# Retuning a planned instruction order: nine z buffers, new cost estimates, later table changes, and later state sums in a fused scan, attention and expert kernel

## The chip, the core and the metric

The kernel runs on one core of a Trainium2 chip. The metric is device time in microseconds (us), as the median of several executions. TensorE is called PE here (PEld its weight loads), VectorE DVE, ScalarE ACT, GpSimd POOL, and SyncE SP; SP issues nearly all DMAs.

## What is computed

The input is x, four images (batches) of 384 channels by 32 x 32 points. Two layers follow each other.

```
# layer 0: selective scan over 4 traversals k of the image
xs    = cross_scan(group_norm(x))                       # L = 1024 steps
dt    = softplus(dtw @ (xw_dt @ xs) + bias)             # per channel d
h     = h * exp(dt * A[n]) + (dt * xs) * B[n]           # 16 states n per channel
y     = sum_n h[n] * C[n]  (+ D * xs), merged over the 4 traversals
x     = x + gelu(layer_norm(y))
# layer 1: tokens
t     = t + attention(layer_norm(t))                    # 6 heads, window of 64, causal
t     = t + sum over the top 2 of 4 experts of gate * (gelu(t' w1 + b1) w2 + b2)
```

## The kernel before, in words

**The scan.** One slot of the scan is 128 rows (32 channels by 4 states) by 1024 time steps. There are 768 slots: 4 batches, 4 traversals, 12 blocks of 32 channels, 4 groups of 4 states. For each slot there is a chain:

- `times_b` (L808): POOL multiplies `dtu` (dt times x, spread to 128 rows by a DMA) with the B rows into a buffer `z`.
- `decay` (L824): ACT makes `dA` = exp(dt * A) into PSUM, out of the spread `dts`. There are two `dA` buffers.
- `scan` (L850): DVE runs the recurrence with dA and z. If the planner finds POOL less loaded than DVE, the result goes back into z and POOL multiplies it with C; if not, it goes into dA and DVE multiplies it with C into z (`times_c`, L837).
- `fold_y` (L884): for each pair of slots, once both products with C are ready, four matmuls with `fold` sum the states into PSUM (`ps_y`). After four such pairs DVE adds the running sum `yp`, which is stored again. Only after its fold is a z buffer free.

The spreads `dtu` and `dts` come by `spread` (L798): a 512 KB DMA from a DRAM copy `dtr`, one for each block of 32 channels, and one buffer each; slots alternate between the two blocks of a pair, so two of the four buffers of each kind are in use at a time and two can be loaded ahead. `time_steps` (L741) makes dt with matmuls (`ps_dt`) and ACT's Exp and Ln.

**The tokens and the experts.** When all of a batch is scanned, `tokens` (L961) does attention in tiles of 128 tokens, three at a time, `route` (L1203) picks two experts for each token, and `experts` (L1317) runs 19 blocks of 128 tokens through one expert each: four chunks of 9 matmuls `ps_hid`, three gelus on ACT (`hs`), and 3 matmuls `y_ff`. There are 76 such blocks in all. `combine` (L1409) gathers and adds the result. This work of batch b runs beside the scan of batch b+1 and later; that of the last batch, and what is left over, runs after the scan.

**What sets the order.** All of these are Python generators. The `Machine` (L211) plays them through while the program is built: each operation gets an estimated cost from `Engine.ask` (L154), each engine has a clock, and of the operations that are ready the one with the best time and bias goes out next (`choose`, L322). The chip then runs each engine's instructions in exactly that order, with semaphores between engines; a wrong estimate shows as an engine that waits at the head of its queue. Rules that the change touches:

- PE costs (L177 to L181): 0.00176 us a column; a fold matmul (32 output rows) 0.01 + 0.00022 n; a matmul with fewer than 32 input rows (`ps_dt`) 0.6 of the normal cost. All PE costs grow by `COLD` = 1.9 (L371) while the planned PE load of a stretch of 3.413 us is under a third; `asked.work` (L196) says how much a matmul counts for that load.
- ACT costs (L183): 0.08 + 0.00085 n, and 0.1 more for each operand that is a tensor.
- `PATIENCE` (L369): ACT takes first what needs the function table that is loaded; an operation that needs another table is let in when it has waited this long, or when nothing else is ready. Exp, Ln and Gelu have a table each.
- `settled` (L257): work that asks for it isn't ordered before the planner's clock is within `SOON` = 0.5 us of the time at which its inputs are estimated to be written. `three`, `hidden`, `combine` and `fold_y` (L897) ask for it.
- Stocks of buffers (L511, L512): `NZ` = 7 z buffers, four `dtu` and four `dts`, all of 128 x 1024 float32. `AHEAD` = 3: z is made at most three slots ahead of the scan.

Of the kernel before, what the change touches and what calls it, by code (L numbers as in the profile page):

```python
# [17 lines left out]
P = 128  # L18
B, D, HH, WW = 4, 384, 32, 32
L = HH * WW  # L20
# [22 lines left out]
HID_RANK = 2  # L43
GELU_BIAS = EARLY
FAVOUR = 1.0
TILES, EPS, NZ = 3, 1e-5, 7
CORES = 1
NEG = -1.0e30

# [80 lines left out]
class Engine:  # L130
# [23 lines left out]
    def ask(self, op, a, k):  # L154
        aps = [v for v in list(a) + [v for n, v in k.items() if n not in ("out", "accum_out")] if hasattr(v, "tensor")]
        if "out" in k:
            outs, ins = [k["out"]], aps
        else:
            outs, ins = aps[:1], aps[1:]
        if op == "value_load":  # L160
            outs, ins = [], aps
        if op == "tensor_tensor_reduce":
            outs, ins = outs + ins[-1:], ins[:-1]
        if k.get("accum_out") is not None:
            outs = outs + [k["accum_out"]]
        for v in list(k.values()):
            if isinstance(v, bass.IndirectOffsetOnAxis):
                ins = ins + [v.ap]
        n = max(v.free_size() if callable(v.free_size) else v.free_size for v in (outs if op == "matmul" else outs + ins))
        size, table = 0, None  # L170
        if "dma" in op:
            size = max(_nbytes(v) for v in outs + ins[:1])
            if op == "indirect_dma_start":
                size = P * D * 4
            cost = dict(pool=1.0, act=0.38, sp=0.48)[self.name]
        elif self.name == "pe":
            cost = max(n, 122) * (0.00088 if op == "transpose" else 0.00176)  # L177
            if outs[0].shape[0] == 32:
                cost = 0.01 + 0.00022 * n
            if ins[0].shape[0] < 32:  # L180
                cost *= 0.6  # L181
        elif self.name == "act":
            cost = 0.08 + 0.00085 * n + 0.1 * sum(hasattr(k.get(v), "tensor") for v in ("bias", "scale"))  # L183
            cost += 0.19 if "accum_out" in k else 0.0
            table = TABLES.get(a[2]) if op == "activation" else None
        elif self.name == "pool":
            cost = 0.1 + 0.0022 * n
        elif self.name == "sp":
            cost = 1.5
        else:  # L190
            cost = 0.17 + 0.00198 * n if "scan" in op else 0.14 + 0.00105 * n
            if n < 256 and not any(v.space == PSUM for v in outs + ins):
                cost += 0.5
        asked = Op(self.name, outs, ins, cost, table, size)
        if self.name == "pe":
            asked.work = cost * min(ins[0].shape[0], P) / P if outs[0].shape[0] > 32 else 0.5 * cost  # L196
        return asked


def _nbytes(ap):  # L200
    n = 4
    for s in ap.shape:
        n *= s
    return n
# [6 lines left out]
class Machine:  # L211
# [42 lines left out]
            t = max(t, r + (HOP if e != eng else 0.0))  # L254
        return t

    def settled(self, *tiles):  # L257

        names = [ap.tensor.name for ap in tiles]
        return lambda: max(self.written.get(n, (0.0, None))[0] for n in names) <= self.t + SOON  # L260

    def account(self, op, start):
        e = op.eng
# [102 lines left out]
            raise RuntimeError("tracing is stuck")  # L366


PATIENCE = 3.0  # L369
SOON = 0.5  # L370
WINDOW, COLD = 3.413, 1.9  # L371
MARGIN, QUEUES = 1.0, ("sp",)

# [3 lines left out]
def conv_attn_hybrid(  # L377
# [89 lines left out]
    m = Machine(nc)  # L467
# [41 lines left out]
    work = ctx.enter_context(tc.tile_pool(name="work", bufs=1))  # L509
    rp = ctx.enter_context(tc.tile_pool(name="rp", bufs=2))  # L510
    zs_ = Stock(m, work, "z", NZ, [P, L])  # L511
    dtus, dts = (Stock(m, work, n, 4, [P, L]) for n in ("dtu", "dts"))  # L512
    bs_, cs_ = (Stock(m, work, n, 4, [P, L]) for n in ("rb", "rc"))
    rows = Stock(m, work, "row", NROW, [P, D])
    xbs, xbts, hss, ybs = (
# [334 lines left out]
    def scan():  # L850

        for s in range(NSLOT):
            n, g = place_of(s)
            i = blocks[n][0]
            yield lambda: s in zs and s in das
            z, da = zs[s], das.pop(s)
            on_pool = count_of["times"] >= min(s + AHEAD, NSLOT) and m.clock["pool"] < m.clock["dve"] + LEAD
            h = z if on_pool else da
            if turns[i][1] >= 2:
                yield from dve.tensor_tensor_scan(  # L860
                    h[:, ::-1], da[:, ::-1], z[:, ::-1], 0.0, ALU.mult, ALU.add
                )
            else:
                yield from dve.tensor_tensor_scan(h, da, z, 0.0, ALU.mult, ALU.add)
            count_of["scan"] = s + 1
            if s % SP == 0:
                m.spawn(fold_y(n), EARLY)
            if on_pool:
                das_.give(da)
                m.spawn(times_c(s, h, True))  # L870
            else:
                yield from times_c(s, h, False)
        ended.append(True)
        yield lambda: len(das_.free) == 2
        for stock in (banks, ybank):
            stock.free.append(das_.free.pop(0))
        for stock, n in ((zs_, NZ), (dts, 4), (dtus, 4)):
            yield lambda: len(stock.free) == n
            rows.free += stock.free
            stock.free = []  # L880
# [3 lines left out]
    def fold_y(n):  # L884


        i, t, j = blocks[n]
        b, k = turns[i]
        rows_y = ydr[b][t, j : j + 2].rearrange("j r l -> (j r) l")
        prev = yield from yps.take("yp")  # L890
        yield from sp.dma_start(prev, rows_y)
        ps = None
        for g in range(NG):
            s = n // 2 * SP + 2 * g
            yield lambda: s in ready and s + 1 in ready
            pair = zs[s], zs[s + 1]
            yield m.settled(*pair)  # L897
            mm = Calls()
            if ps is None:
                ps = yield from banks.take("ps_y", 0)  # L900
            for n_z, z in enumerate(pair):
                for h in range(2):
                    if k % 2:
                        rhs = z.rearrange("p (w h) -> p w h", h=HH)[:, :, ts(h, HH // 2)]
                    else:
                        rhs = z[:, ts(h, LH)]
                    q = 32 * (2 * n_z + h)
                    mm.matmul(ps[q : q + 32, :], fold, rhs, start=g == 0, stop=g == NG - 1)
            yield from pe.all(mm)
            zs_.give(zs.pop(s), zs.pop(s + 1))  # L910
        yield from dve.tensor_tensor(prev, ps, prev, ALU.add)
        if k == LAST_BY_COLUMNS:
            yield from act.copy(
                ps.rearrange("p (h w) -> p w h", w=WW), prev.rearrange("p (w h) -> p w h", w=WW)
            )
            yield from act.copy(prev, ps)
        banks.give(ps)
        yield from sp.dma_start(rows_y, prev)
        yps.give(prev)
        folded[b] = folded.get(b, 0) + 2  # L920
        if folded[b] == KG * NB:
            have.add(("scan", b))
# [618 lines left out]
```

## Time and profile before

| | us |
|---|---|
| median of 3 runs | 4078.01 (4070.57 to 4080.3) |
| the profiled execution | 4065.49 |
| its span in the trace | 4063.8 |
| busy PE / DVE / ACT / POOL | 3014.8 / 2878.0 / 2432.7 / 2855.7 |
| first scan starts / last scan ends | 104.1 / 3140.3 |
| mean granted PE clock | 0.804 |

The profile has a page with busy time of each engine, the span cut into 40 slices with the busy share of each engine in tenths (9 is 90% or more), and groups of instructions with their count, busy time, mean duration in ns, and the idle time just before them. Further views of the same trace list who waited for whom, busy time in chosen stretches, and single instructions in order of time. Almost every instruction has line L141 or L152 (the two helpers that record operations), so groups are told apart by their tiles: `z<-dts,bc` is an instruction that writes z and reads dts (or dtu) and a row tile. A float32 matmul stands as two records (a transpose as one). Idle time of an engine is put down to what released it last; it costs only where that engine is the one that others wait for.

### The profile page before, as it was taken

The numbers are of one execution on the slowest core, as the hardware profiler recorded it, in microseconds if no ns is written. First come the engines' busy times: TensorE is split into PE (matmuls) and PEld (weight loads), VectorE is DVE, ScalarE is ACT, GpSimd is POOL, SyncE is SP. The second block draws the span as 40 slices with busy tenths as digits, with TensorE's granted clock in tenths as the row PEclk, the third lists the DMA queues.
The fourth block names the chain that finished last, engine by engine and source line by source line (L and its number), as shares of the span: only waits on it lengthen the run. The fifth ranks groups of instructions, "written<-read, shape, count | busy, mean of one in ns | idle before, by whom it ended". The sixth has DMA issues, their size and how long they took to land. (4 is left out here: it accounts for less than half of the span.)

```text
span 4063.8 us, 49234 instructions
## 1 busy us (share of the span) xinstructions
PE 3014.8 (74%) x15856; PEld 1854.0 (46%) x15856; DVE 2878.0 (71%) x3064; ACT 2432.7 (60%) x3979; POOL 2855.7 (70%) x1490
## 2 busy tenths in 40 slices
PE   3554455576674888677777786767799999998998
PEld 1000000043441455445454444444466788887886
DVE  2999999998889888888888889888897232101001
ACT  3554455476774798777776787877777345222221
POOL 1999989989897789999987899899997110101001
PEclk8555566577775899878877787887799999998997
DMA  5565564634345989464668795664569754998995
GB/s 200 203 250 209 217 209 151 209 109 162 114 154 184 382 315 355 164 229 140 215 209 283 268 358 195 230 197 171 190 243 337 240 170 142 345 335 295 315 317 193
DMA packets 368570, 935.11 MB, mean 230 GB/s; under 512 B 48372, under 2 KB 160120, under 8 KB 368312
## 3 DMA queue, kind: packets, MB, share of 16 engines
q1 hardware_dynamic: 360120, 906.79, 63.6%
q0 software_dynamic: 8192, 25.17, 1.8%
q8 instruction: 126, 2.06, 0.2%
q14 instruction: 132, 1.08, 0.1%
HBM read 786.39 MB, written 164.30 MB: 234 GB/s over the span
## 5 line engine op out<-in xcount | busy, mean ns | idle before, releaser
L141 POOL TENSOR_TENSOR z<-dts,bc 128x1024 f32<-128x1024 f32 x768 | 1792.2, 2358 | 177.7 <-PE ps_y L152 95.3
L141 ACT ACTIVATE dA<-dts,a 128x1024 f32<-128x1024 f32 x768 | 851.1, 1116 | 485.5 <-DVE z L141 456.6
L152 PE MATMUL ps_y<-z,fold 128*32 128x512 f32 x3072 | 734.9, 806 | 536.1 <-POOL z L141 253.6
L141 DVE TENSOR_TENSOR_SCAN dA<-dA,z 128x1024 f32<-128x1024 f32 x393 | 899.1, 2288 | 107.6 <-ACT dA L141 88.6
L141 POOL TENSOR_TENSOR z<-z,bc 128x1024 f32<-128x1024 f32 x375 | 879.6, 2356 | 102.6 <-DVE z L141 99.7
L141 DVE TENSOR_TENSOR_SCAN z<-dA,z 128x1024 f32<-128x1024 f32 x375 | 843.8, 2276 | 41.2 <-ACT dA L141 39.4
L152 PEld LDWEIGHTS ps_hid<-xbt,w_sb 128*128 128x128 f32 x5472 | 682.1, 201 | 132.5 <-issue 25.7
L152 PE MATMUL ps_hid<-xbt,w_sb 128*128 128x128 f32 x5472 | 702.0, 286 | 38.0 <-ACT dt L141 19.4
L152 PE MATMUL y_ff<-w_sb,hs 128*128 128x384 f32 x1824 | 659.7, 500 | 19.2 <-ACT hs L141 15.2
L141 ACT ACTIVATE hs<-ps_hid,bb 128x128 f32<-128x128 f32 x912 | 270.5, 366 | 457.1 <-PE ps_hid L152 351.6
L152 PEld LDWEIGHTS ps_y<-z,fold 128*32 128x32 f32 x3072 | 95.1, 123 | 971.4 <-POOL z L141 466.2
L141 ACT ACT_TABLE_LOAD x388 | 497.8, 1283 | 17.2 <-issue 3.6
L141 DVE TENSOR_TENSOR z<-dA,bc 128x1024 f32<-128x1024 f32 x393 | 479.8, 1221 | 13.0
L152 PEld LDWEIGHTS y_ff<-w_sb,hs 128*128 128x128 f32 x1824 | 331.7, 195 | 240.5 <-issue 47.5
L141 POOL DMA_INDIRECT cb<-ysdr,idx x64 | 61.7, 963 | 441.6 <-issue 281.7
L141 DVE COPY xbt<-ps_xb 128x384 f32<-128x384 f32 x39 | 21.7, 556 | 407.7 <-PE ps_xb L152 407.7
L152 POOL TENSOR_TENSOR rn<-rn,half 128x1 f32<-128x1 f32 x96 | 52.5, 547 | 265.6 <-DVE rn L152 256.2
L141 POOL DMA_INDIRECT xsdr<-tks,idx x64 | 63.9, 999 | 168.9 <-DMA xsdr<-tks,idx 119.5
L152 PE MATMUL ps_dt<-xd,dtw_sb 12*128 12x512 f32 x192 | 99.8, 856 | 45.9 <-ACT dt L141 19.2
L152 PE MATMUL ps_o<-v,pt 128*128 128x64 f32 (+1 forms) x720 | 110.1, 315 | 19.6 <-DVE tt L141 7.2
L141 ACT COPY dt<-ps_sp 128x512 f32<-128x512 f32 x96 | 56.0, 584 | 113.5 <-DVE e L141 113.2
L152 PEld LDWEIGHTS ps_o<-v,pt 128*128 128x128 f32 (+1 forms) x720 | 104.9, 227 | 29.4 <-DVE tt L141 7.7
(189 smaller groups left out, 3219.4 us busy)
## 6 DMA issues: line engine op xcount, KB each, us to landing
w_sb<-wl SPq DMA_DIRECT2D x608, 576.0 KB
dts<-dtr SPq DMA_DIRECT2D x384, 512.0 KB
bc<-xdr SPq DMA_DIRECT2D x128, 512.0 KB
ub<-udr SPq DMA_DIRECT2D x48, 512.0 KB
dtr<-e SPq DMA_DIRECT2D x48, 512.0 KB
dtr<-dt SPq DMA_DIRECT2D x48, 512.0 KB
yp<-ydr SPq DMA_DIRECT2D x96, 256.0 KB
ydr<-yp SPq DMA_DIRECT2D x96, 256.0 KB
```

The source lines that it names most:

```text
L141: return getattr(self.real, op)(*a, **k)
L152: getattr(self.real, op)(*a, **k)
```

## The change

Seven things change, most of them inside the planner.

1. `NZ` goes from 7 to 9, and `dtu` and `dts` from 4 to 3 buffers each, so the memory is the same.
2. A fold matmul is estimated at 0.02 + 0.0004 n instead of 0.01 + 0.00022 n, which for its 512 columns is 0.225 us instead of 0.123 us.
3. A matmul with fewer than 32 input rows is estimated at 0.9 of the normal cost instead of 0.6.
4. An ACT operation is estimated at 0.1 + 0.00088 n instead of 0.08 + 0.00085 n, and a fold counts for 0.7 of its cost instead of 0.5 in the planned PE load.
5. `PATIENCE` goes from 3 to 5 us.
6. `fold_y` asks `settled` with `sure` = 1.5: the four matmuls are ordered only when the planner's clock is 1.5 us past the estimated end of both products, where it was 0.5 us ahead of it. The other users of `settled` keep 0.5 us ahead.
7. At the end of the scan the buffers are handed to the later stages in their new numbers.

```diff
-TILES, EPS, NZ = 3, 1e-5, 7
+TILES, EPS, NZ, SURE = 3, 1e-5, 9, 1.5
...
             if outs[0].shape[0] == 32:
-                cost = 0.01 + 0.00022 * n
+                cost = 0.02 + 0.0004 * n
             if ins[0].shape[0] < 32:
-                cost *= 0.6
+                cost *= 0.9
         elif self.name == "act":
-            cost = 0.08 + 0.00085 * n + 0.1 * sum(hasattr(k.get(v), "tensor") for v in ("bias", "scale"))
+            cost = 0.1 + 0.00088 * n + 0.1 * sum(hasattr(k.get(v), "tensor") for v in ("bias", "scale"))
...
-            asked.work = cost * min(ins[0].shape[0], P) / P if outs[0].shape[0] > 32 else 0.5 * cost
+            asked.work = cost * min(ins[0].shape[0], P) / P if outs[0].shape[0] > 32 else 0.7 * cost
...
-    def settled(self, *tiles):
+    def settled(self, *tiles, sure=-0.5):
 
         names = [ap.tensor.name for ap in tiles]
-        return lambda: max(self.written.get(n, (0.0, None))[0] for n in names) <= self.t + SOON
+        return lambda: max(self.written.get(n, (0.0, None))[0] for n in names) <= self.t - sure
...
-PATIENCE = 3.0
-SOON = 0.5
+PATIENCE = 5.0
...
-    dtus, dts = (Stock(m, work, n, 4, [P, L]) for n in ("dtu", "dts"))
+    dtus, dts = (Stock(m, work, n, 3, [P, L]) for n in ("dtu", "dts"))
...
-        for stock, n in ((zs_, NZ), (dts, 4), (dtus, 4)):
+        for stock, n in ((zs_, NZ), (dts, 3), (dtus, 3)):
...
             pair = zs[s], zs[s + 1]
-            yield m.settled(*pair)
+            yield m.settled(*pair, sure=SURE)
```

## The prediction

> **What bounds the kernel now.** I read the page's slices first, to find the stages, then busy time by stages, then what the engine that sets the pace waited for.
>
> ```profile
> PE   3554455576674888677777786767799999998998
> DVE  2999999998889888888888889888897232101001
> ACT  3554455476774798777776787877777345222221
> POOL 1999989989897789999987899899997110101001
> ```
>
> A slice is 101.6 us. For 31 slices DVE and POOL are nearly full; then they fall idle and PE is at nine tenths to the end. So the time is a sum of two stages: the scan, to the end of its last instruction at 3140.3 us, and a tail of 4063.8 - 3140.3 = 923.5 us in which PE is the bound. I cut the scan at each 96 slots (from the start of its first scan at 104 us):
>
> ```profile
> core 0: us, PE busy (x) PEld busy (x) DVE busy (x) ACT busy (x) POOL busy (x), PEclk, DMA share, GB/s
> ...
> 106.00:433.00 327.00, 164.60 (x410) 22.68 (x410) 316.46 (x215) 175.32 (x196) 312.25 (x137) 0.54 0.64 226
> 433.00:779.00 346.00, 178.30 (x466) 27.24 (x464) 331.07 (x230) 178.05 (x190) 322.13 (x141) 0.59 0.52 183
> 779.00:1176.00 397.00, 268.63 (x1323) 150.53 (x1322) 347.76 (x401) 272.55 (x460) 361.18 (x195) 0.72 0.43 148
> 1176.00:1577.00 401.00, 293.47 (x1579) 175.72 (x1577) 344.15 (x306) 296.89 (x418) 336.96 (x159) 0.82 0.77 285
> ...
> 3140.00:4064.00 924.00, 879.12 (x5479) 714.09 (x5477) 141.25 (x447) 279.79 (x818) 90.49 (x121) 0.96 0.76 262
> ```
>
> The first two stretches hold the scan alone: DVE is idle for 10.5 and 14.9 us of them, which is what lies between its instructions. From 779 on, tokens and experts run beside the scan, ACT's work rises, and DVE is idle for 49 and 57 us a stretch. What DVE waited for between 106 and 3140 us:
>
> ```profile
> DVE dA L141 <- ACT dA L141: 88.6, 68, 3.8
> DVE yp L141 <- PE ps_y L152: 39.5, 29, 3.7
> DVE z L141 <- ACT dA L141: 39.4, 35, 3.6
> ...
> DVE dA L141 <- POOL z L141: 12.5, 9, 6.3
> ```
>
> The columns are total us, times, longest. DVE waits 128.0 us for dA from ACT, 110 us for PE (39.5 for the state sums, the rest attention tiles), and only 12.5 us for z from POOL. So DVE sets the pace of the scan, with ACT next to it. POOL waits too: 99.7 us for DVE and 95.3 us for z buffers that a fold holds. But as DVE hardly ever waits for POOL, that is POOL's own slack.
>
> **The change, step by step.** The planner alone decides what the edits do, so I counted the two built programs' instructions, engine by engine, up to the last scan and after it, and priced the differences by rows of this profile.
>
> *Work that leaves the scan on DVE.* 382 products with C are on DVE instead of 393, and 386 instead of 375 on POOL. 11 x 1.221 us (the row of z<-dA,bc) = 13.4 us less on DVE and 11 x 2.356 = 25.9 us more on POOL, which has the slack above. The routing of one batch moves behind the scan, some 55 instructions of 0.17 to 0.2 us, 10 us, and a few copies, 2 us. Together **-25 us** on the engine that sets the pace.
>
> *Table changes put off.* 49 fewer ACT_TABLE_LOADs in the scan (320 for 369), and 58 fewer gelus there.
>
> ```profile
> L141 ACT ACT_TABLE_LOAD x388 | 497.8, 1283 | 17.2 <-issue 3.6 <-PE ps_g L152 3.5 <-DVE yp L141 1.7
> ```
>
> 49 x 1.283 = 62.9, 58 gelus at 0.29 us (0.88 us for three in the timeline) = 17, copies 6: 86 us less on ACT. ACT is not the bound, so this counts only through DVE's waits. In the six loaded stretches DVE idles 49, 57, 61, 49, 43 and 41 us against 13 in the empty ones, 224 us more, while ACT is busy 705 us more in all: 0.32 us of DVE idle for one of ACT. 86 x 0.32 = **-27 us**. Ends: 0 (if the waits come from the bursts that stay), and -86.
>
> The Trainium skill, "ScalarE: Activation LUTs", section on what ACT_TABLE_LOAD costs, gives 1283 ns for the load and about 1380 ns more for a drain. The trace has the first and not the second: at 1500.21 us a load begins and the gelu after it starts at 1501.51. By the page ACT would lose 153 us and DVE gain 49; I keep 27.
>
> *Folds ordered later, priced higher.* On the chip four folds took 1.06 us warm (3099.80 in the timeline), where the planner had 0.49 and now has 0.90. DVE's wait for `yp` comes right behind a fold, so a later planned end should take some of it. PE itself waits 401 us at folds for z (253.6 for POOL, 147.4 for DVE), and this should shrink; but of the 222 us that ACT waits for PE in the scan only 17 fall together with a wait of PE at a fold, and of DVE's 110 only 12. I take half of the 39.5 us: **-20 us**; ends 0 and -110. Nothing is queued on PE behind a fold that DVE needs soon but these tiles; a later fold holds two z buffers 2 us longer, and the two new buffers, at 3140/768 = 4 us of scan a slot, cover that twice.
>
> *Three spread buffers.* With three, the second block of the next pair can only be loaded when the first of the present pair is done. In the program of before, at least 23.6 us of POOL's work lay between the last use of a buffer and the first use of what is loaded into it, and 10.0 us of ACT's. Now 23 of 192 loads of `dtu` have under 5 us of POOL's work and 33 of 192 of `dts` under 5 us of ACT's. A load takes, from the row that shows it, 5.4 us: the first one is issued at 90.27 and POOL starts at 95.67. Before, POOL waited once, 2.1 us, for such a load. POOL's lateness is covered by the three slots that it runs ahead. ACT's exps are paced by DVE (456.6 us of waiting for it), so that three slots, 10 us or more, usually pass. I take **+10 us**. Ends: 0 and +120 (the rival below).
>
> *The tail.* After the last scan the changed program has 180 more `ps_hid` matmuls and 57 more `y_ff`: 20 and 19 more chunks, five expert blocks that no longer fit beside the scan, since folds, `ps_dt` and gelu waits are now dearer in the plan. In the timeline of the tail chunks of 9 and 3 matmuls follow each other:
>
> ```profile
> 3157.17 2.17 PE L152 MATMUL ps_hid<-xbt,w_sb 128*128 128x128 f32 x18
> ...
> 3159.18 2.10 PE L152 MATMUL y_ff<-w_sb,hs 128*128 128x384 f32 x6
> ...
> 3161.12 2.17 PE L152 MATMUL ps_hid<-xbt,w_sb 128*128 128x128 f32 x18
> ```
>
> 3161.12 - 3157.17 = 3.95 us a chunk; 19.5 x 3.95 = 77, four more turned inputs at 0.55 = 2, six `ps_c` and five folds, 3: **+82 us**. PE is busy 879 of the tail's 924 us, so nothing hides this; the ends are +70 and +95. In the scan these blocks lay beside DVE's work and cost only what they took from ACT, which is counted above.
>
> *The sum*: 4063.8 - 25 - 27 - 20 + 10 + 82 = 4083.8 us of span. The execution lies 1.7 us above its span, so 4085.5. The profiled execution, 4065.49, is 12.5 us below the median of the runs shown, 4078.01; carried over, **4098 us**, 0.5% slower. The scan would end at 3078 us instead of 3140.
>
> **The rivals.**
>
> *A truer plan takes the waits away (faster).* What DVE waits for in the scan is 128.0 + 110.2 = 238 us. If estimates close to the chip's durations halve all of it, -119 stands in place of -27 and -20, with no cost of the spreads: 4063.8 - 25 - 119 + 82 = 4001.8, so 4016 us. It decides from 82 - 25 = 57 us on, a quarter of the waits. For it: folds were estimated at under half of their time, and exps at 1.05 us where the row has 1.116 (1.10 now). Against: the costs of DVE, POOL and of attention's matmuls, which stand behind most of these waits, are not touched.
>
> *The spreads come late (much slower).* If SP stands waiting at its head when a buffer comes free, as it did for `yp` 53 times with 276.5 us, 5.2 us each, then a tight `dts` load is 5.4 + 5.2 - 3 (its room) - 4 (the spare dA) = 3.6 us late: 33 x 3.6 = 120 us in place of 10: 4194 us of span, so 4208. It decides when more than a few tens of exps wait for a DMA.
>
> *It evens out (no change).* The scan gains what the tail loses, 82 us; this lies between the forecast and the first rival, 4078 us. The change then does on each engine what it says and the end stays.
>
> **Chances.** Forecast 0.42, its own range 4065 to 4130; truer plan 0.30; late spreads 0.13; evens out 0.15. The two outer ends are long, so the range that should hold 8 in 10 goes from 3995 (the truer plan with some more than half of the waits) to 4185 (late spreads at two thirds). About 0.3%, 12 us, is what a measurement here can tell from no change: faster 0.33, same 0.14, slower 0.53.
>
> **What would show it.** The time of the last scan's end (3078 forecast, under 3058 for the first rival); PE busy time after it (82 us more); DVE's waits for dA (100 us or so against 128) and for `ps_y` (20 against 39.5); waits of ACT or POOL for `dts<-dtr` (few, or some 30 in the second rival); POOL's 95.3 us for `ps_y` should fall with nine buffers, without worth. I am wrong if DVE's idle time in the loaded stretches falls by more than a third, or if the tail costs less for a block than here.

## The result, and the profile after

The changed kernel took 4084.36 us (median of 14 runs, 4076.81 to 4099.13), the kernel before 4073.44 us (14 runs, 4065.28 to 4080.3): a ratio of 1.0028, 95% interval 1.0016 to 1.0039. It is slower by 0.16 to 0.39%, some 11 us, where the forecast was 20. The profiled execution took 4093.43 us, its span 4091.7, the mean granted PE clock 0.788 against 0.804.

The slices of the changed kernel's page, in tenths of busy time; a slice is now 102.3 us:

```profile
PE   3444454476665687778687868678899899998998
DVE  2999999999898988889898798998881232101001
ACT  3555465466765687777677777777772344222221
POOL 1999999899998999999887899999991110101001
```

The shape is the same, but DVE and POOL leave off one slice earlier. Busy time of the changed kernel, cut at each 96 slots and at the end of the last scan:

```profile
core 0: us, PE busy (x) PEld busy (x) DVE busy (x) ACT busy (x) POOL busy (x), PEclk, DMA share, GB/s
106.00:431.00 325.00, 157.76 (x410) 23.82 (x410) 318.37 (x217) 175.10 (x196) 314.03 (x138) 0.54 0.66 229
431.00:768.00 337.00, 162.66 (x456) 26.64 (x456) 328.49 (x230) 177.91 (x190) 319.94 (x140) 0.58 0.53 188
768.00:1141.00 373.00, 249.26 (x1190) 140.58 (x1190) 342.77 (x373) 251.63 (x420) 355.35 (x185) 0.68 0.44 152
1141.00:1529.00 388.00, 277.11 (x1328) 152.38 (x1327) 348.86 (x340) 265.20 (x373) 356.85 (x175) 0.76 0.69 247
...
3062.00:4091.00 1029.00, 975.95 (x5971) 790.14 (x5970) 161.25 (x517) 291.48 (x867) 97.31 (x130) 0.94 0.76 262
```

All stretches but one got shorter (373 us for 397, 388 for 401; the sixth went from 408 to 418). The first three hold no expert block in either kernel, as the first block starts at 1339 us in the kernel before; so the gain is not only one of blocks that left. The scan ends at 3061.8 us for 3140.3, so it gave 78.5 us; the tail lasts 1030 us for 923.5, so it took 106 us, and PE is busy 976 us of it for 879. From the first scan to the end of the last, DVE's busy time fell from 2711 to 2684 us and its idle time from 325.6 to 272.9; 30 of these 53 us lie in the first 288 slots, ahead of any expert block. DVE's waits between 106 and 3140 us in the changed kernel (total us, times, longest; the 78 us behind its scan add 0.4 us to the row of `yp` and nothing to the other three):

```profile
DVE dA L141 <- ACT dA L141: 72.1, 57, 4.0
...
DVE z L141 <- ACT dA L141: 39.3, 37, 3.0
DVE yp L141 <- PE ps_y L152: 24.6, 15, 9.7
DVE dA L141 <- POOL z L141: 20.9, 10, 6.4
```

DVE's waits for ACT's dA fell by 16.5 us in the first line and those for the state sums by 15, waits for POOL rose by 8. All waits for PE in the scan went from 110.3 to 86.8 us. POOL's and ACT's waits for the spreads, from the same kernel's waits up to 3062 us:

```profile
POOL z L141 <- DVE z L141: 58.3, 26, 5.0
...
POOL z L141 <- DMA dts<-dtr: 18.4, 11, 4.2
POOL z L141 <- PE ps_y L152: 11.0, 6, 2.6
```

POOL's 95.3 us for buffers that a fold holds became 11.0. The spreads do come late now, 11 times for POOL and 10 times (33.8 us) for ACT. Little of it reaches DVE: right behind ACT's ten late exps it waited at five of them for that dA, 7.7 us in all.

One thing in the tail was not in the forecast. In the kernel before, 10 of the 16 indirect scatters of the third batch's routing had started by the end of the scan, and the last started 35 us behind it (at 3175.7 us). Now all 16 come after the scan. POOL's timeline after the last scan begins like this (start, us, instruction, idle time before it):

```profile
3084.93 1.04 POOL L141 DMA_INDIRECT xsdr<-tks,idx  x1 [20.45 <-DVE idx L152]
3090.09 0.99 POOL L141 DMA_INDIRECT xsdr<-tks,idx  x1 [4.12 <-DMA xsdr<-tks,idx]
...
3179.07 0.97 POOL L141 DMA_INDIRECT xsdr<-tks,idx  x1 [6.12 <-DMA xsdr<-tks,idx]
3180.06 0.59 POOL L152 TENSOR_TENSOR rn<-rn,half 128x1 f32<-128x1 f32 x1
```

Each scatter waits for the one before it to land, 4.1 us and more, so the row of them holds POOL until 3180, and the last batch's first `rn` stands behind it. ACT waits 20.26 us for that `rn`, and PE once 11.3 us behind ACT; PE's only longer wait in this tail is one of 14.4 us at its end, where the kernel before has one of 14.2 us.

### The profile page after: what moved, and what is told of

Its sections match the earlier page's. It is cut to its first block, busy times and chain, and to the rows that moved or that the text cites. A ratio compares the mean times of both kernels' runs of the same rounds, so it can differ in the third digit from the quotient of the medians.

```text
span 4091.7 us, 49091 instructions
## 1 busy us (share of the span) xinstructions
PE 3039.7 (74%) x15850; PEld 1887.5 (46%) x15850; DVE 2872.0 (70%) x3069; ACT 2358.1 (58%) x3905; POOL 2879.0 (70%) x1501
## 5 line engine op out<-in xcount | busy, mean ns | idle before, releaser
L152 PE MATMUL ps_y<-z,fold 128*32 128x512 f32 x3072 | 700.6, 809 | 500.1 <-POOL z L141 254.8
L141 POOL TENSOR_TENSOR z<-z,bc 128x1024 f32<-128x1024 f32 x386 | 906.8, 2358 | 58.7 <-DVE z L141 58.3
L141 DVE TENSOR_TENSOR_SCAN dA<-dA,z 128x1024 f32<-128x1024 f32 x382 | 874.0, 2288 | 94.3 <-ACT dA L141 72.1
L141 DVE TENSOR_TENSOR_SCAN z<-dA,z 128x1024 f32<-128x1024 f32 x386 | 867.4, 2276 | 40.2 <-ACT dA L141 39.3
L152 PE MATMUL ps_hid<-xbt,w_sb 128*128 128x128 f32 x5472 | 696.1, 285 | 29.8 <-ACT dt L141 7.7
L141 DVE TENSOR_TENSOR z<-dA,bc 128x1024 f32<-128x1024 f32 x382 | 466.4, 1221 | 11.8
L141 ACT ACT_TABLE_LOAD x340 | 436.2, 1283 | 20.2 <-PE ps_g L152 9.9
L141 DVE COPY yb<-y_ff 128x384 f32<-128x384 f32 x31 | 17.2, 553 | 198.7 <-PE y_ff L152 177.5
L152 PE MATMUL ps_s<-k,q 64*128 64x192 f32 (+1 forms) x384 | 99.2, 413 | 33.9 <-ACT dt L141 16.5
```

The costliest lines, as they stand in the source:

```text
L141: return getattr(self.real, op)(*a, **k)
L152: getattr(self.real, op)(*a, **k)
```

## The experiments

Three theories. **A**: the prediction's own sum, each term at its price. **B**: its first rival; PE's estimates lie nearer to the chip, and that takes DVE's waits away. **C**: its third rival, that it evens out, put as a mechanism: DVE's idle time in the scan is the price of the expert blocks that run beside it, so each block that leaves takes its idle time along.

All results together. Ratio is to the kernel before on the same chips, with its 95% interval; scan end, DVE's idle time in the scan and the tail are from one profiled execution each, in us; blocks are the expert blocks that the built program has ahead of the last scan (36 `ps_hid` matmuls are one).

| kernel | median us | ratio | blocks | scan end | DVE idle | tail |
|---|---|---|---|---|---|---|
| before | 4073.44 | 1 | 35.0 | 3140.3 | 325.6 | 923.5 |
| changed | 4084.36 | 1.0028 (1.0016 to 1.0039) | 30.0 | 3061.8 | 272.9 | 1030.0 |
| e1 PE's estimates undone | 4079.76 | 1.0013 (0.9996 to 1.0029) | 33.6 | 3136.7 | 324.4 | 941.8 |
| e2 PE's estimates alone | 4124.06 | 1.0119 (1.0101 to 1.0138) | 31.1 | 3133.9 | 299.7 | 985.1 |
| e3 routing beside tokens | 4081.85 | 1.0023 (1.0009 to 1.0037) | 30.0 | 3058.8 | 268.8 | 1017.2 |
| e4 five blocks left out | 4015.36 | 0.9853 (0.9832 to 0.9875) | 30.0 | 3066.5 | 274.6 | 944.5 |
| e5 buffers alone | 4087.7 | 1.0024 (1.0011 to 1.0038) | 33.2 | 3130.1 | 326.2 | 963.4 |
| e6 patience alone | 4090.07 | 1.0033 (1.0019 to 1.0046) | 34.7 | 3148.9 | 335.6 | 935.5 |
| e7 late folds undone | 4110.07 | 1.0067 (1.0044 to 1.0091) | 29.8 | 3084.9 | 282.1 | 1027.8 |
| e8 less PE work in the tail | 4060.89 | 0.9961 (0.9947 to 0.9975) | 30.0 | 3061.4 | 270.3 | 997.4 |
| e9 before, blocks held back | 4152.1 | 1.0173 (1.015 to 1.0195) | 30.0 | 3146.2 | 334.4 | 1013.6 |
| e10 late folds alone | 4123.22 | 1.0106 (1.0083 to 1.0129) | 31.2 | 3127.2 | 292.4 | 996.4 |
| e11 buffers undone | 4107.15 | 1.0067 (1.0045 to 1.0088) | 30.5 | 3103.5 | 281.9 | 1001.9 |
| e12 patience undone | 4140.14 | 1.0143 (1.012 to 1.0167) | 27.1 | 3062.9 | 273.4 | 1073.4 |
| e13 late folds, buffers | 4073.25 | 0.9994 (0.9983 to 1.0006) | 33.5 | 3134.0 | 322.6 | 941.0 |
| e14 PE's estimates, patience undone | 4116.77 | 1.0104 (1.0085 to 1.0122) | 32.8 | 3147.6 | 357.4 | 961.9 |
| e15 old fold price | 4062.74 | 0.9961 (0.9947 to 0.9976) | 33.0 | 3115.2 | 311.2 | 949.3 |
| e16 old short matmul price | 4050.84 | 0.9945 (0.9925 to 0.9965) | 31.3 | 3060.9 | 281.1 | 996.4 |
| e17 fold price alone of the three | 4076.23 | 0.9992 (0.9976 to 1.0007) | 32.7 | 3101.4 | 305.1 | 970.0 |
| e18 lower short matmul price | 4052.06 | 0.9941 (0.9921 to 0.9961) | 33.8 | 3117.2 | 329.4 | 943.2 |

Single executions of one kernel spread by some 20 us, so a stage of one profile is good to about 10 us, and the ratios decide. Where runs are subtracted below, the ratios are, at 0.1% for 4.1 us.

**e1.** The changed kernel, with PE's three estimates as before.

```diff
-                cost = 0.02 + 0.0004 * n
+                cost = 0.01 + 0.00022 * n
...
-                cost *= 0.9
+                cost *= 0.6
...
-            asked.work = ... else 0.7 * cost
+            asked.work = ... else 0.5 * cost
```

> The changed kernel with PE's three estimates (fold, few input rows, planned load) as before; the rest of the change stays. By the order of its instructions 129 hidden matmuls and 42 output matmuls (14.2 chunks) return from the tail into the scan, the routing of the third batch too, with 12 table loads more, and 5 products with C fewer on DVE than in the changed kernel. Theory A (time = scan end + tail; the tail at 3.95 us a chunk, the scan by DVE's work and a third of ACT's): tail 56 us shorter and 10 to 20 more without the late routing, scan about 13 us longer, so 4084 - 55 to - 65 = about 4025 us, faster than both. Theory B (dearer PE estimates make the plan true and so take DVE's waits away): the scan end goes back by most of the 53 us of idle time that it had won, 4075 to 4085 us.

Measured 4079.76. The scan went back to its old end, 3136.7, and DVE's idle time to 324.4, with 37 table loads fewer than before and with the late folds still in. So A falls for the scan: neither ACT's relief nor the late order alone carried it. Without the estimates most blocks are back beside the scan and the tail is 18 us over that of before. The time is that of B, but as 3.6 blocks came back too, C would also have the idle time rise; this run does not part the two.

**e2.** The kernel before, with those three estimates new, nothing else.

> The kernel before with PE's three estimates of the change alone. 142 hidden and 45 output matmuls (15.4 chunks) move from the scan into the tail; 16 products with C more on DVE, 9 table loads fewer. Theory A: tail + 61 us, DVE + 20 us, ACT's relief - 8 us: 4073 + 73 = about 4145 us, clearly slower. Theory B: the waits of DVE go down by 40 to 50 us, about 4095 us or less.

Measured 4124.06, 1.2% slower: DVE's idle time fell by 26 us, its work rose by 18 and the tail by 62. The time lies between A (4145) and B (4095 or less). The idle time fell by half of what the whole change takes, but four blocks left the scan with it, so that C explains it as well; alone, these estimates cost far more in the tail.

**e3.** The changed kernel, with the third batch's scatters sent off beside the last batch's tokens instead of ahead of them.

```diff
-        yield from m.together([scatter(a) for a in range(NT)], 4, EARLY)
-        routed[b] = xs, idx, p, eid, gate
+        def send():
+            yield from m.together([scatter(a) for a in range(NT)], 4, EARLY)
+            routed[b] = xs, idx, p, eid, gate
+        if b == 2:
+            m.spawn(send(), EARLY)
+        else:
+            yield from send()
```

> The changed kernel, the same to the end of the scan; after it the scatters of the third batch's routing run beside the next batch's attention instead of ahead of it, so that only 8 of 16 stand ahead of its first norms on POOL. Theory C (the routing that moved behind the scan holds attention up by POOL's queue of scatters, and PE then idles 11 us and runs at a lower granted clock for some 300 us): 11 to 25 us faster than the changed kernel, about 4060 to 4073 us, the granted clock between 100 and 400 us after the scan at 0.95 or more. If the tail is only a matter of chunks: no change, 4084 us.

Measured 4081.85, 0.05% under the changed kernel with overlapping intervals; its profiled tail is 13 us shorter. The granted clock in the three hundreds of us behind PE's 11.3 us wait was 0.88, 0.88 and 0.91 in the changed kernel, and 0.98 in each from 100 us behind the scan here, as expected. So the moved routing is visible in one trace, but by the medians it costs 2 us, and not more than some 10 by their intervals.

**e4.** The changed kernel without the last batch's last five blocks: their tokens pass through unchanged.

```diff
+        MBC = MB - 5 if b == B - 1 else MB
...
             for o in range(MB):
+                if o >= MBC:
+                    xb = yield from xbs.take("xb")
+                    yield from sp.dma_start(xb, xs[ts(o, P), :])
+                    yield from sp.dma_start(ysdr[b][ts(o, P), :], xb)
+                    xbs.give(xb)
+                    left.append(o)
+                    continue
...
-            for o in range(MB):
+            for o in range(MBC):
...
-            for o in range(MB):
+            for o in range(MBC):
```

> The changed kernel, the same to the end of the scan; of the last batch the last five blocks of the expert layer are left out (their weights aren't loaded, their inputs are passed on as outputs). Theory A with the price that the prediction used: 20 chunks at 3.95 us and 5 turned inputs at 0.55, 82 us, so about 4002 us. If a block costs more than the chunks (stalls between blocks, weights that come late): 100 us or more, under 3985 us.

Measured 4015.36: 1.75% or 71 us under the changed kernel, give or take 10 by the two intervals, so 14 us a block (12 to 16). The forecast priced a block at 82 / 5 = 16.4.

**e5.** The kernel before with the buffers alone.

```diff
-TILES, EPS, NZ = 3, 1e-5, 7
+TILES, EPS, NZ = 3, 1e-5, 9
...
-    dtus, dts = (Stock(m, work, n, 4, [P, L]) for n in ("dtu", "dts"))
+    dtus, dts = (Stock(m, work, n, 3, [P, L]) for n in ("dtu", "dts"))
```

> The kernel before with nine z and three of each spread buffer, nothing else. The plan moves with it: 40 table loads and 22 gelus fewer in the scan, 10 products with C fewer on DVE, 64 more ps_hid matmuls (7 chunks) in the tail. Theory A (the prices of the prediction): DVE work -13, ACT 58 us x 0.32 = -18, spreads +10, tail 7.1 x 3.95 = +28: 7 us slower than before, some 4080. Theory B (only better estimates of PE take DVE's waits away, buffers and table changes do not): DVE stays idle for 315 to 330 us in the scan, -13 and +25 remain: 4085. Theory C (buffers are what the plan lacked): idle under 300 us, 4060 or less.

Measured 4087.7, 10 us slower, between A and B. Forty table loads fewer, and DVE's idle time is 326.2 as before; it fell from 77 to 54 us in the first 288 slots and rose as much behind them. C, in the form that buffers were missing, falls for the scan as a whole.

**e6.** The kernel before with `PATIENCE = 5.0` for 3.0.

> The kernel before with a patience of 5 us instead of 3, nothing else: 28 table loads and 6 gelus fewer in the scan, 11 more ps_hid matmuls in the tail. Theory A: ACT 28 x 1.283 + 4 = 40 us x 0.32 = -13, tail 1.2 chunks +5: 4065. Theory B (the table loads stood in ACT's slack, and gelus that wait longer hold PE up): DVE's idle time in the scan stays above 320 us, 4073 to 4078.

Measured 4090.07, 13 us slower: worse than both theories. DVE's waits from 106 to 3149 us:

```profile
DVE dA L141 <- ACT dA L141: 60.3, 55, 3.8
DVE yp L141 <- PE ps_y L152: 53.9, 38, 6.0
...
DVE dA L141 <- POOL z L141: 25.0, 18, 3.5
```

Waits for dA did fall, from 88.6 in this line to 60.3 with 28 table loads fewer, and the waits for `yp` and z took their place, 39.5 to 53.9 and 12.5 to 25.0. Here the wait that went only uncovered what was late next.

**e7.** The changed kernel with the early folds again: `SURE` -0.5 for 1.5.

> The changed kernel with folds ordered as early as before (half a microsecond ahead of the estimated end of both products), all else kept. Tables 318 against 320 in the scan, one chunk more in the tail, about 2 us less of products on DVE. If the later order took the waits for yp and PE away (the prediction's 20 us): waits for yp back from 24.6 to 35 us or more, POOL and PE wait at each other, 4095 or more. If the estimates did it alone: waits for yp stay under 28 us, 4084 to 4088.

Measured 4110.07, 16 us over the changed kernel (0.39%). DVE's waits for `yp` went back to 34 us and PE's at folds for POOL from 255 to 330 us, as expected of the late order, but DVE's idle time rose by 9 us only; the rest is 14 us of work on DVE.

**e8.** The changed kernel, where the last five blocks load all their weights and do less with them.

```diff
                     for j in range(HT):
+                        if b == B - 1 and o >= MB - 5 and c:
+                            mm.matmul(ps[:, ts(j, P)], w[:, j * P : j * P + P],
+                                      xts[o][:, ts(0, P)], start=True, stop=True)
+                            continue
...
                     for j in range(HT):
+                        if b == B - 1 and o >= MB - 5 and c in (1, 2) and j:
+                            continue
```

> The changed kernel, where the last five expert blocks of the last batch load all their weights, but leave out 90 ps_hid and 20 y_ff matmuls (so part of the experts' sum is missing). If PE is the bound of the tail: 90 x 0.223 + 20 x 0.65 = 33 us less, 4051. If the weights' DMAs are (DMA share 0.92 to 0.95 in the tail): 0 to 8 us less, 4076 to 4084. In between, each end of a chunk waits for what is later, and a chunk costs less than 3.95 us of PE.

Measured 4060.89, 0.67% or 27 us under the changed kernel, give or take 7, of an estimated 33 us of PE work left out. PE bounds the tail, and not the weights' DMAs, which would have given 0 to 8 us; whether a part of PE's relief goes to other waits can't be told within these intervals.

**e9.** The kernel before, with its blocks held to the starts that the changed kernel's plan has.

```diff
+STARTS = [347, 353, 360, 368, 373, 381, 388, 394, 416, 434, 468, 520, 539, 545, 551, 559, 564, 571, 577, 596, 619, 641, 657, 672, 695, 724, 732, 746, 755, 761]
...
                 for c in range(NCH):
+                    if not c and b * MB + o < 35:
+                        yield scans((STARTS + [NSLOT] * 5)[b * MB + o])
                     hs = yield from hss.take("hs")
```

> The kernel before, with every estimate, buffer and rule as it was, but its expert blocks held back: none begins before the slot at which the plan of the changed kernel begins it, and the five that the changed kernel leaves for the tail wait for the end of the scan. In the scan it has the work of before on DVE (1 product with C more), 35 table loads and 58 gelus fewer. Theory B (better estimates of PE took DVE's waits away): DVE's idle time in the scan falls only by ACT's relief, 64 us x 0.32 = 20, to 300 us or more; tail +69 to +82: 4121 to 4135. Theory C (idle time in the scan is the price of the blocks that run beside it, some 10 us for each, whatever the estimates are): idle 285 us or less, like the 273 of the changed kernel; tail the same: 4090 to 4105.

Measured 4152.1, 1.7% slower. Busy time in its scan and tail, with the columns of the table by stretches above, then DVE's waits up to 3146 us (the helpers' lines are one further down here):

```profile
106.00:3146.00 3040.00, 2078.49 (x9849) 1086.65 (x9849) 2705.57 (x2553) 2060.79 (x3034) 2742.62 (x1338) 0.73 0.61 212
3146.00:4160.00 1014.00, 964.08 (x5943) 781.39 (x5939) 144.89 (x453) 294.70 (x870) 95.48 (x126) 0.95 0.77 264
```

```profile
DVE dA L142 <- ACT dA L142: 85.7, 57, 5.7
DVE z L142 <- ACT dA L142: 42.4, 39, 3.6
DVE yp L142 <- PE ps_y L153: 42.0, 35, 6.5
...
DVE dA L142 <- POOL z L142: 16.4, 10, 4.8
```

ACT has 58 us less to do than before (2060.79 for 2118.68), PE 25 us less, five blocks have left the scan, and DVE waits as long as ever: 42.0 for `yp`, 85.7 for dA, idle 334.4.

How far this carries shows by stretches. Up to 1339 us, where the kernel before starts its first block (slot 323), PE, ACT, DVE, POOL and SP have the same instructions in the same order as before. Still, the first 288 slots took 13 us longer here, with 12 us more of DVE's idle time (89 for 77). The third and fourth stretch of this run, to compare with the prediction's rows for 779 to 1176 and 1176 to 1577 us:

```profile
781.00:1191.00 410.00, 281.71 (x1331) 164.31 (x1332) 347.15 (x401) 274.52 (x466) 362.48 (x195) 0.68 0.42 143
1191.00:1574.00 383.00, 251.58 (x1194) 129.05 (x1193) 345.69 (x309) 249.90 (x338) 336.04 (x159) 0.74 0.70 250
```

So 12 us are what two executions of one order differ by. From slot 288 on, the scan is 7 us shorter than before and DVE idle for 246 us for 249. The fourth stretch, which lost 3.7 of the five blocks, did lose idle time, 55 to 37 us, and the later ones took nearly all of it back. C wanted some 40 us less over the scan, and A's price for ACT's relief wanted 20; neither shows, though the 12 us of noise leave the smaller one less certain. What the blocks cost behind the scan is some 70 us by the ratio (61 to 79), 14 each, or up to 15 if the 7 us are real.

**e10.** The kernel before with the late folds alone (`settled(*pair, sure=1.5)`).

> The kernel before with the folds ordered 1.5 us behind the estimated end of both products, nothing else. The plan moves with it: 13 products with C more on DVE, 28 table loads and 46 gelus fewer in the scan, 138 more ps_hid matmuls (3.8 blocks) in the tail. By the prediction's prices: DVE +16, ACT 49 x 0.32 = -16, folds -10 (half of the 20), tail 15.3 x 3.95 = +60: 4123. Theory C: DVE +16, blocks out of the scan -40, in the tail 3.8 x 13.8 = +53: 4102. With seven z buffers POOL's wait for buffers that a fold holds grows over 95 us; if DVE's wait for POOL grows with it (over 30 us), it is dearer still.

Measured 4123.22, 43 us slower by the ratio where the prices gave 50. DVE's idle time fell by 33 us, its work rose by 20 and the tail by 73. First POOL's waits, then DVE's for POOL, up to 3127 us:

```profile
POOL z L141 <- PE ps_y L152: 156.3, 66, 10.0
POOL z L141 <- DVE z L141: 53.5, 32, 6.3
```

```profile
DVE dA L141 <- POOL z L141: 38.1, 20, 5.2
```

With seven z buffers a late fold makes POOL wait 156 us for them (95.3 before), and DVE for POOL 38.1 (12.5 before). Here the buffers count.

**e11.** The changed kernel with seven z and four of each spread buffer.

> The changed kernel with seven z and four of each spread buffer again, all else kept. 30 products with C more on DVE, 6 table loads more, half a block less in the tail. By the prediction's prices: DVE +37, tail -8, ACT +2, spreads -10: some 21 us slower than the changed kernel, 4105. If the spreads that come late cost more than the 10 us (29.5 us of ACT's and POOL's waits for dts each hit DVE): 4085 to 4095. If the late folds need the buffers: POOL waits over 95 us for them and DVE for POOL over 35: 4110 or more.

Measured 4107.15, 16 us over the changed kernel where the prices gave 21. POOL's and DVE's waits up to 3104 us show the same as e10:

```profile
POOL z L141 <- PE ps_y L152: 104.7, 61, 7.2
POOL z L141 <- DVE z L141: 92.0, 40, 9.5
```

```profile
DVE dA L141 <- POOL z L141: 41.0, 21, 8.5
```

DVE's wait for POOL is 41.0 against 20.9, and 30 products went back to DVE, whose busy time rose by 32 us. That work is most of the 42 us by which the scan ends later. A relief of 10 us by the fourth spread buffer is not to be seen.

**e12.** The changed kernel with `PATIENCE = 3.0`.

> The changed kernel with a patience of 3 us again, all else kept. Table loads 330 for 320, 2 products fewer on DVE, 104 more ps_hid matmuls (2.9 blocks) in the tail. By the prediction's prices: DVE -3, tail 11.5 x 3.95 = +46: 43 us slower than the changed kernel, some 4127. Theory C (a block costs DVE 10 us beside the scan and 13.8 behind it): -30 and +40, 4094; DVE's idle time in the scan falls to some 245 us.

Measured 4140.14, 1.15% or 47 us over the changed kernel; A had 43, C 10. Three blocks more left the scan, DVE's idle time stayed at 273.4 (C wanted 245), and the tail took it all: 47 us for 2.9 blocks, 16 each.

**e13.** The kernel before with late folds and the buffers.

> The kernel before with late folds, nine z and three of each spread buffer; estimates and patience as before. 4 products fewer on DVE, 18 table loads fewer in the scan, 53 more ps_hid matmuls (5.9 chunks) in the tail. If late folds take DVE's waits for PE away wherever buffers allow it (as alone, 33 us): DVE idle 295 us or less, -5 -33 + 23 = -15 against before, some 4060, faster than both kernels. If late folds need the estimates of PE too: idle 315 us or more, 4085 to 4095.

Measured 4073.25, no difference from before. DVE's idle time is 322.6, so late folds do not take 33 us wherever buffers allow it. The two plans also differ in blocks, 33.5 beside the scan here and 31.2 in e10, which C would count as some 23 us.

**e14.** The changed kernel with PE's estimates and the patience of before.

> The changed kernel with PE's three estimates and the patience of before: late folds, buffers and ACT's estimate stay. 29 products with C fewer on DVE, tables as before, 81 more ps_hid matmuls (9 chunks) in the tail. By the prices: DVE -35, tail +36. If the longer patience was what ate the gain of late folds: DVE idle 300 us or less, 25 us faster than before, 4050. If late folds give nothing without PE's estimates: idle 320 or more, 4070 to 4080.

Measured 4116.77, 42 us slower, against both expectations. DVE's work fell by 25 us (35 were counted) and its idle time rose to 357.4, the highest of all. Patience was not what ate the gain; why this plan is so much worse stays open.

**e15.** The changed kernel with the fold's old price: `cost = 0.01 + 0.00022 * n`.

> The changed kernel with the fold's old price (0.123 us a matmul) alone put back. 8 more chunks than before in the tail (+32), DVE's products -11, tables 330. If the fold's price carries the gain: DVE idle 315 us or more, 4085 to 4095. If the price of the short matmuls or the fold's share in the planned load does: 290 us or less, 4055 to 4065.

Measured 4062.74, 0.39% faster than before. The time is that of the second case, but idle 311.2 lies between the two marks: with the old price and the new share a part of the waits is gone.

**e16.** The changed kernel with the old price of short matmuls: `cost *= 0.6`.

> The changed kernel with the old price of matmuls with fewer than 32 input rows (0.6 of the normal cost) alone put back. 15 more chunks than before in the tail (+59) and one routing (+10), DVE's work -28. If this price carries the gain: DVE idle 310 us or more, 4100 or more. If the fold's price does: idle 275 us or less as in the changed kernel, 4060 to 4070.

Measured 4050.84, faster than before by 0.35 to 0.75% and than the changed kernel by 34 us. Busy time in scan and tail:

```profile
108.00:3061.00 2953.00, 2058.21 (x9926) 1108.57 (x9927) 2671.82 (x2487) 2044.22 (x3024) 2771.09 (x1347) 0.74 0.63 220
3061.00:4058.00 997.00, 948.93 (x5864) 769.57 (x5862) 155.66 (x509) 294.63 (x861) 99.81 (x133) 0.95 0.77 267
```

The scan ends where that of the changed kernel ends, with 1.3 blocks more beside it, and the tail is 34 us shorter. The dearer short matmuls had pushed work behind the scan and given nothing for it there. At 14 to 16 us a block that is some 20 of the 34 us; the rest is not accounted for.

**e17.** e16 with the fold's old share, `0.5 * cost`: the fold's price is then the only new one of PE's three.

> The changed kernel with the old price of the short matmuls and the fold's old share (0.5) in the planned load: of PE's three estimates only the fold's price is new. Against the run before (old short matmul price alone): routing back in the scan (+10) and 4 products more (+5) on DVE, 5.7 chunks less and no routing in the tail (-22 -13). If the fold's price carries the gain: DVE idle 295 us or less, 20 us faster than that run, 4030. If the share in the load does: idle 315 us or more, 4060 to 4075.

Measured 4076.23, the time of before and 19 us over e16. Idle 305.1 is again between the marks: with the new price and the old share, too, only a part of the waits is gone.

**e18.** e16 with short matmuls cheaper still, `cost *= 0.5`.

> The changed kernel with short matmuls at 0.5 of the normal cost, below the 0.6 of before; the fold's price and share stay new. Against the run with 0.6: routing back in the scan and 6 products less on DVE (+3), 10 chunks less and no routing in the tail (-40 -13). If this price only moves blocks: DVE idle 295 us or less, 4005 to 4020. If blocks that come back beside the scan bring DVE's waits back: idle 315 us or more, 4045 to 4065.

Measured 4052.06, as fast as e16 and as e16 faster than both kernels. It has 2.5 blocks more than e16 beside the scan; the tail fell by 53 us and the scan's end rose by 56, its idle time to 329.4. That is the second case: with blocks back beside the scan DVE's waits are back, as C has it and unlike e9. Past e16 the exchange is even.

**Read together.** Of the plans listed, leaving out e3, e4 and e8, which keep the changed kernel's scan, seven have the fold's new price and its new share in the planned load (changed, e2, e7, e11, e12, e16, e18): DVE's idle time is 273 to 329 us, mean 289. Eight have neither (before, e1, e5, e6, e9, e10, e13, e14): 292 to 357, mean 327. The two with one of them lie between, 305 (e17) and 311 (e15). So 39 us go with price and share. The late order makes no such difference within the groups (means 288 with it and 291 without among the first, 324 and 330 among the second), nor does patience (289 with 5 us and 287 with 3 among the first).

That the 39 us come from price and share is not shown, for the groups differ in blocks too: 30.5 beside the scan on the mean in the first, 33.0 in the second. At like numbers of blocks most of the difference is gone: 281 and 300 us (e16, e2, with 31.3 and 31.1 blocks) against 292 (e10, 31.2), and 329 (e18, 33.8) against 324 and 323 (e1, e13, 33.6 and 33.5). By a straight line through the fifteen plans without e9 and e14, idle time rises by 9.5 us a block with a scatter of 9 us, which is C's price; through all seventeen it is 8.7 with a scatter of 18. Against C stand e9 (30.0 blocks, 334) and e12 (three blocks fewer than the changed kernel, the same idle time), and the first 288 slots, where no plan has a block yet: there the means are 53 us in the first group and 68 in the second, and in the second 75 with seven z buffers and 61 with nine. So blocks, PE's estimates and buffers each go along with DVE's waits, and these runs do not part their shares.

## Why the prediction was right or wrong

- **The two stages, and their signs**: right. The scan's end was forecast at 3078 us and came at 3061.8; the tail was forecast 82 longer and is 106 longer. Neither outweighs the other by much, in the forecast as on the chip.
- **DVE's work, -25**: 2711 to 2684, -26 before rounding. Right.
- **Table changes, "86 x 0.32 = -27"**: this step failed; it is the cost in DVE's idle time that the sum put on ACT's work. ACT's busy time did fall by 87 us, but the factor 0.32 came from comparing stretches with and without expert work, in which everything else differs too. With ACT relieved and PE's estimates as before, DVE's idle time did not fall: e9 (58 us less on ACT) +9, or -3 from slot 288 on, as the orders are the same up to slot 323; e5 (40 loads fewer) +1; e6 (28 fewer, the edit that does little else) +10, and the kernel 13 us slower where this price had it 8 faster. The lower end, 0, fits these three. The prediction read the six loaded stretches as tokens and experts together, but the third has no expert block and still 51 us of DVE's idle time.
  The Trainium skill, "ScalarE: Activation LUTs", section on what ACT_TABLE_LOAD costs, adds a drain to each load. This trace does not show the drain: behind nine in ten of the loads of either kernel the next instruction of ACT starts 1.3 us after the load's start. The larger gain, which the prediction estimated from it at 49 us, is not seen either.
- **"I take half of the 39.5 us: -20"**: the wait for `yp` did become 24.6, the size forecast, but waits for dA and for other PE results moved with the plan too, not `yp` alone. What this term, the table changes and the spreads promised together was 37 of idle time, and 53 were measured, 30 of them ahead of the first expert block. That the scan's end came near its forecast is in part luck: one term without a gain that shows, and gains elsewhere that no term had.
- **The first rival** (a truer plan takes the waits away) had the wrong size, and its mechanism is neither shown nor excluded: DVE's waits for ACT's dA and for PE fell by 39 of the 238 us (to 112.5 and 86.8), a sixth and not a half, below the 57 from which it decides. "The costs of DVE, POOL and of attention's matmuls are not touched" was the reason against it, and it agrees with the size.
- **Spreads, +10**: late 21 times with 52 us in all, of which 7.7 reached DVE by way of ACT; the second rival did not happen. But the nine z buffers were said to be "without worth". Together with late folds they are worth 16 us (e11): without the two, DVE waits 41 us for POOL and the plan puts 30 products back on it. Alone, they cost 10 us (e5).
- **The tail, 19.5 x 3.95 = 77, with the rest +82**: this term was too large, by little more than the intervals. By the medians the five blocks are worth 71 us (e4, 61 to 81) or 70 (e9), 14 each for 16.4; e12 has 16. "If the tail costs less for a block than here" was one of the prediction's signs of being wrong; the other, a third less idle time in the loaded stretches, did not come (300 to 258). The profiled tail grew by more, 106 us; 13 of that is the routing (e3), which the forecast counted as 10 us less on DVE and not as 16 scatters ahead of the last batch's `rn` on POOL's queue. Its cost by the medians is 2 us.
- **From 4098 to 4084.4**: 4.6 us are the base, as the median of three runs, 4078.01, was that much over the median of 14. The other 9 us are the change itself, +20 forecast and +11 measured: with 71 + 2 for the tail in place of 82, the forecast's scan of -62 gives just that, but this part is worked out and not measured by itself. The two profiles have +28 us, as the one of before was one of the quickest executions, 8 us under its median, and the one of the changed kernel 9 us above. A difference of two single profiles could not have told +20 from +11.

**What stays open**: what shares the blocks that left, PE's estimates and the buffers have in the 53 us that DVE no longer waits, and why e14 is so slow. Each edit reorders the whole plan, and plans that differ by one constant differed by 10 to 30 us of idle time without a single place to point at. Sums by the prediction's prices held within 10 us for e5, e10, e11 and e12, where counted work and blocks are the largest terms; where a gain in DVE's idle time was to decide, the first expectation of e1, e2, e6, e13 and e14 missed by 13 to 67 us.

## What to carry to other kernels

In a kernel whose order is planned while it is built, an estimate changes two things: how long engines wait, and what still fits beside the bound engine. Count the second from the built programs, since each unit that drops into a serial tail has a price (14 to 16 us a block here), and try each estimate by itself: one of three, for matmuls that hardly matter, cost the 34 us that turned a gain into a loss (e16). A ratio of idle time to busy time read across stages is no price; take the load away alone, as e9 does, before you count on it. When many plans are sorted into two groups, look for what else differs between the groups.

## What the runs showed of the hardware

- Indirect scatters into one tensor that wait for each other are slow: 0.97 us of POOL each, but 5.2 to 8.0 us from the start of one to the next in the tail, 94 us for 16.
- PE, busy 95% of the tail, gave back 27 us, give or take 7, of some 33 us of matmuls that were taken from it (e8), with its DMA at a share of 0.76.
- Fewer table loads by 28 to 40 at 1283 ns each, on an engine that is busy 70% of the scan, shortened the scan by no more than the change of DVE's work in e5, e6 and e9 (-10, +9 and +6 us). Each of these reorders the plan as well.
- One profiled execution can lie 9 us to either side of the median, with a granted clock of 0.804 in one and 0.788 in the other; for changes below half a per cent that is as much as the effect.
- The same instructions in the same order took 1074 us in one execution and 1087 in another (the first 288 slots of before and e9), at a granted clock of 0.72 and 0.68 in the last third of them.
